# Two attention layers over 64 small graphs: the first step's turn moved from TensorE to VectorE and transfers, and the first loads reordered

## The chip, the core and the metric

The kernel runs on one core of a Trainium2 chip. A core has five engines with instruction streams of their own: TensorE (PE, matrix products and transposes, with PEld its weight loads), VectorE (DVE), ScalarE (ACT), GpSimd (POOL) and SyncE (SP), which here only issues transfers (DMAs). SyncE and ScalarE issue DMAs; 16 DMA engines carry them out. The metric is the device time of one launch in microseconds (us), lower is better. A time is compared as the median of several runs.

## What is computed

Input x holds 64 graphs of 256 nodes with 512 features, all in float32; adj holds a 256 x 256 adjacency of booleans for each graph. Two layers follow each other, both of the form x = x + attention(relu(layernorm(x))).

```
# layer 0: 4 heads of 64
h = relu(layernorm(x)); q, k, v = h @ Wq, h @ Wk, h @ Wv          # 512 -> 256 each
sim = where(adj, q k^T / 8, -max); x = x + softmax(sim) v @ Wo + bo
# layer 1: 8 heads of 64
h = relu(layernorm(x)); h = layernorm(h) * gamma + beta
q, k, v = split(h @ w_qkv.T)                                      # 512 -> 512 each
s = where(adj | eye, q k^T / 8, -1e9); x = x + softmax(s) v @ w_out.T + b_out
```

## The kernel before

**Steps and periods.** `fast_path` works on two graphs at a time: a step has G = 2 graphs of 256 rows, so NT = 4 row blocks of 128 rows, and there are NSTEP = 32 steps. The large products are done by a scheme with seven products for a 2 x 2 block product (`PRODUCT`, `project_qk`, `project_v1`, `combine`); its sums of operands (`act_sums0`, `act_sums1`, `weight_sum`) are made mostly by GpSimd.

**Who sets the order.** Nothing is scheduled automatically: TensorE, VectorE, ScalarE and GpSimd run in the order in which the program emits instructions, and that order is written by hand. `at(period, place, fn, ...)` puts a call at a place on a common scale (a period is 6.4 long, 6.2 where its number is negative), and at the end all events are sorted by place and called (L1496). Each engine takes its instructions from this list in that order, and an instruction that waits holds up all that stand behind it on its engine. SyncE's transfers come in the same order, and SyncE waits in order too. Transfers use eight completion semaphores in turn, so one transfer is issued only when the one eight places before it has landed.

**Start of the kernel.** Steps 0 and 1 are brought in by a path of their own, before the regular rhythm begins:

- `first_loads` (L432) loads x of step 0 in four row blocks with Wq, Wk, the flags of step 0 and Wv. `load_h(1)` (L505) loads step 1's x, 1 MB, into a buffer of the tag "xt" of the pool io.
- `norm0` (L665) takes mean and variance of each row block on VectorE (L647, L648); GpSimd makes the factor r (L677 for step 0, `row_scales` L657 to L659 for the others). `first_scale` (L685) and `scale_row` (L661) apply them on ScalarE (L689, L663). Their place in step 0 is by row block.
- `first_turn` (L791, TensorE) and `first_fill` (L803) turn step 0's h and write the ReLU into hT. Each of the four column chunks is evacuated by ScalarE if even and by VectorE if odd (L807, L809). `first_qk` (L811, L820) projects q and k; VectorE (L827) and ScalarE (L828) evacuate.
- `neighbours` (L581, L587) finds on VectorE which rows have any neighbour (the flags, any_of); `adjacency_cast` (L543) and `adjacency_transpose` (L547) turn the adjacency with TensorE for steps 0 to 2; `neighbours_rows` and `neighbours_turn` (L606, L614) spread the flags.
- **The turn of h.** hT must have the features on the partitions. There are two ways. `transpose_h` (L728) lets TensorE transpose 16 blocks of 128 x 128 (L735), and ScalarE evacuates each chunk with the ReLU (L739). `turn_blocks` (L754) and `move_blocks` (L764) let VectorE transpose 32 x 32 blocks in place (L759, four instructions) and then move the blocks between partitions by 16 transfers of 64 KB issued by SyncE (L771); `place_h` (L773) then applies the ReLU on ScalarE from SBUF (L782, four instructions, each needs all 16 transfers). `by_tensor` (L749) chooses: TensorE for step 0, for step 1 of layer 0 and for the last step of layer 1, the transfers for all others.
- Behind the turn, step 0's attention of layer 0 is done pair by pair (a pair is two heads): `scores` (L1055), `mask_scores` (L1078), `exponentials` (L1083), `weigh` (L1126), `weigh_out` (a copy by ScalarE, L1141). The four score banks of PSUM are used in turn. The sums of each pair's exponentials are made by GpSimd and VectorE (L1090, L1096, L1103), inverted in `key_sums` (L1159), written to DRAM (`line`, L1173, 4 KB) and read back spread over the partitions by `inverse_in` (L1184, two transfers a pair); GpSimd multiplies them in (`normalise`, L1202). `combine_rows` (L1018, L1025) then multiplies with w_o, after both pairs.
- Step 1's first projection (`project_qk`, L902) runs between step 0's pair 0 and its combine.
- **Weights.** `weight_load` (L473) loads w_qkv in three parts (n = 0, 1, 2 for q, k, v; four blocks each of 256 KB in rows of 512 bytes, L481) and w_out (n = 3, one transfer of 1 MB, L478). VectorE turns w_qkv (`weight_turn`, L490), TensorE w_out (`weight_block`, L498). `later_weights` (L451) loads w_o in two transfers (L453) and the two bias rows (L458).

SyncE's order at the start is: step 0's loads, step 1's x, w_q (two blocks), step 1's flags, the rest of w_q, w_k, w_out, w_o in two, b_o, b_out, w_v, line of pair 0, x of step 0 again (xt, L524), the two L1184 of pair 0, x of step 2 (L512), flags of step 2, line of pair 1 and its two L1184.

Of the kernel before, what the change touches and what calls it, by code (L numbers as in the profile page):

```python
# [8 lines left out]
FP = mybir.dt.float32  # L9
# [3 lines left out]
AF = mybir.ActivationFunctionType  # L13
# [305 lines left out]
def fast_path(  # L319
# [21 lines left out]
    nc = tc.nc  # L341
    P = 128
    B, N, D = x.shape
    DH = 64
    G = 2
    NSTEP = B // G
    NIC = N // P
    NT = G * NIC
    T = G * N
    NC = D // P  # L350
# [7 lines left out]
    act = ctx.enter_context(tc.tile_pool(name="act", bufs=1))  # L358
# [73 lines left out]
    def first_loads():  # L432
# [12 lines left out]
        for i in range(2):  # L445
# [2 lines left out]
                wv[:, i * P:(i + 1) * P].rearrange("(c p) o -> p c o", p=P),  # L448
            )

    def later_weights():  # L451
        for i in range(2):
            nc.sync.dma_start(  # L453
                wo0[:, 2 * i:2 * i + 2].rearrange("p j c o -> p (j c) o"),
                wo[:, i * HD:(i + 1) * HD].rearrange("(c p) o -> p c o", p=P),
            )
        for v, t in ((bo, bo_b), (b_out, bout_b)):
            nc.sync.dma_start(t, bass.AP(tensor=v.tensor, offset=v.offset, ap=[[0, P], [1, D]]))  # L458

    def first_gamma():  # L460
        gbr = sm.tile([2 * NC, P], FP, name="gbr", tag="turned_p", bufs=1)
# [223 lines left out]
    def first_scale(t):  # L685
        st = S[0]
        r, mr = st["r"][:, t:t + 1], st["mr"][:, t:t + 1]
        nc.vector.tensor_scalar(mr, st["mean"][:, t, 0:1], r, -1.0, op0=ALU.mult, op1=ALU.mult)
        nc.scalar.activation(st["h"][:, t, :], st["h"][:, t, :], AF.Identity, bias=mr, scale=r)  # L689

# [55 lines left out]

    def by_tensor(s, lyr):  # L749

        return s == 0 or s == (1, NSTEP - 1)[lyr]


    def turn_blocks(s, lyr, t):  # L754

        st = S[s]
        if "blocks" not in st:
            st["blocks"] = act.tile([P, NQ, NC, NT, Q], FP, name="blocks", tag=("turned", "h")[lyr])
        nc.vector.transpose(  # L759
            st["blocks"][:, :, :, t, :].rearrange("p b c n -> p c b n"),  # L760
            st["h"][:, t, :].rearrange("p (c b n) -> p c b n", c=NC, b=NQ),
        )
# [39 lines left out]
    def first_fill(g):  # L802
        for c in range(NC):  # L803
            b0, _, step = B_OF[c // HC]
            dst, src = S[0]["hT"][:, b0 + g * step, c % HC, :], S[0]["ph"][c][:, g]
            if c % 2:
                nc.vector.tensor_scalar(dst, src, 0.0, None, op0=ALU.max)  # L807
            else:
                nc.scalar.activation(dst, src, AF.Relu)  # L809
# [402 lines left out]
    def at(period, place, fn, *args):  # L1212
        events.append((period * (PERIOD if period >= 0 else FIRST) + place, len(events), fn, args))
# [93 lines left out]
    for s in range(NSTEP):  # L1307
# [2 lines left out]
        if s == 1:  # L1310
            p -= 3.93 / FIRST
        if s:
            at(*((-3, 5.71), (-2, 5.3))[s - 1] if s < 3 else (p - 1, AT_H1 + 0.01), load_h, s)
            at(*((-2, 3.2), (-2, 5.35))[s - 1] if s < 3 else (p - 1, 1.3), load_adjacency, s)
        if s < 3:
            at(p, (2.0, 2.4, -5.95)[s], adjacency_cast, s)
            at(p, (3.46, 3.583, -5.825)[s], adjacency_transpose, s)
        else:
            at(p - 1, 4.9, adjacency_pack, s)
        for t in range(NT):  # L1320
            at(p, ((0.5, 0.9, 1.73, 1.74)[t], (1.6995, 1.6996, 2.0295, 2.0296)[t], -6.3 + 0.01 * t)[s] if s < 3 else (0.95, 1.05, 1.2, 1.35)[t], norm0, s, t)
            if s == 0:
                at(p, (0.95, 1.35, 1.745, 2.15)[t], first_scale, t)
            else:
                at(p, (2.375 + 0.001 * t, (-5.8, -5.799, -5.6, -5.599)[t])[s - 1] if s < 3 else 1.6 + 0.001 * t, scale_row, s, t)
            if not by_tensor(s, 0):
                at(p, AT_X - 0.00035 + 0.00001 * t if s > 2 else (2.6, 2.601, 2.72, 2.721)[t], turn_blocks, s, 0, t)
        if not by_tensor(s, 0):
            at(p, AT_X - 0.00031 if s > 2 else 3.0, move_blocks, s)
        for g in range(G):  # L1330
            if s < 3:
                at(p, (1.8, 2.03, -5.8)[s] + 0.001 * g, neighbours, s, g)
            else:
                at(p - 1, AT_Q0 - 0.0009, neighbours, s, g)
        if s < 2:
# [22 lines left out]
        else:  # L1358
            for c in range(NC):
                if by_tensor(s, 0):  # L1360
                    at(p, 2.9292 + 0.0001 * c, transpose_h, s, 0, c)
                else:
                    at(p, AT_Q0 - 0.001 + 0.0001 * c, place_h, s, 0, c)
            at(p, AT_Q0 - 0.0005 if s > 1 else FIRST_C0 + 0.1, lambda s=s: act_sums0(S[s]["hT"]))
            at(p, AT_Q0 - 0.0004 if s > 1 else FIRST_C0 + 0.101, lambda s=s: act_sums1(S[s]["hT"]))
            at_set(p, 3.3 if s < 2 else AT_Q0, SET, project_qk, s, 0, 0)
# [106 lines left out]
    gbr, blocks = [], {}  # L1473
    at(-3, 5.7, first_loads)
    at(-3, 5.705, lambda: gbr.append(first_gamma()))
    at(-2, 4.93, later_weights)
    for i in range(4):
        at(-2, 4.301 if i else FIRST_Q0 + 0.32, weight_sum, nc.gpsimd, wqk0, i)
        at(-1, 1.21, weight_sum, nc.gpsimd, wo0, i)
    for n, place in ((0, 4.0), (1, 4.0), (3, 4.0), (2, 5.0)):  # L1480
        at(-2, place, lambda n=n: blocks.update({n: weight_load(n)}))
    at(-2, FIRST_V0 + 0.2, lambda: gamma_beta(gbr[0]))
    for i in range(12):
        place = (
            4.6395, 4.6396, 4.9, 4.901, 4.902, 5.19965, 5.19966, 5.7, 12.6, 12.601, 12.602, 13.0,
        )[i]
        at(-2, place, lambda i=i: weight_turn(blocks[i // 4], i // 4, i % 4))
    for c in range(4):
# [53 lines left out]
```

## Time and profile before

| what | us |
|---|---|
| median of three runs (lowest, highest) | 3075.1 (3072.61, 3076.8) |
| the profiled execution | 3072.65 |
| its span, first to last instruction | 3070.9 |
| TensorE busy | 3063.4 |
| VectorE, GpSimd, ScalarE busy | 2534.3, 2295.8, 1212.2 |

The profile is that of one execution. Its page gives busy times, the chain of waits that ended last, and groups of instructions by source line (L735 is line 735). The trace answers finer questions: the chain in order of time in a window, the instructions of one engine in order of time, rates of transfer in a window, and how long a transfer took from issue to landing. TensorE's granted clock is full in all slices of the page. Idle time of an engine that is not on the chain costs nothing by itself.

### The profile page before, as it was taken

To read this page: it belongs to the slowest core of one execution; us is meant where nothing else is said; L and a number is where in the kernel's file an instruction comes from. 1 tells how busy PE (TensorE), PEld (TensorE's weight loads), DVE (VectorE), ACT (ScalarE), POOL (GpSimd) and SP (SyncE) were. 2 spreads that over 40 slices of the span, in tenths; PEclk is the share of its full clock that TensorE was granted. 3 is DMA by queue.
4 is the path that set the end of the run, shared out by engine and by line. 5 is a ranking of instruction groups with operands and counts; after the bars stand their busy time and mean duration, and the time that the engine had idled before them with its cause. 6 is when DMAs were issued, how large, how long until landed. Compare 5 with 4: busy or idle time off the path is not lost.

```text
span 3070.9 us, 55407 instructions
## 1 busy us (share of the span) xinstructions
PE 3063.4 (100%) x20106; PEld 2527.4 (82%) x20106; DVE 2534.3 (83%) x4739; ACT 1212.2 (39%) x2133; POOL 2295.8 (75%) x2120
## 2 busy tenths in 40 slices
PE   9999999999999999999999999999999999999999
PEld 7888888888888888888888888888888888888887
DVE  7888888888888888888888888888888888888766
ACT  5443443434343343433444333443434344343431
POOL 6877787777877777777877777787777877778753
PEclk9999999999999999999999999999999999999999
DMA  6223222233222331323323233222232222332311
GB/s 159 58 88 95 78 75 85 74 95 95 60 88 71 100 95 53 91 73 94 95 60 90 74 89 94 75 77 80 81 94 83 72 83 74 101 91 56 92 35 50
DMA packets 192365, 251.20 MB, mean 82 GB/s; under 512 B 58264, under 2 KB 84504, under 8 KB 192088
## 3 DMA queue, kind: packets, MB, share of 16 engines
q1 hardware_dynamic: 128800, 180.46, 20.8%
q10 hardware_dynamic: 63288, 67.15, 7.5%
q8 instruction: 161, 2.64, 0.4%
q14 instruction: 116, 0.95, 0.1%
HBM read 128.59 MB, written 34.34 MB: 53 GB/s over the span
## 4 chain that ended last, share of the span: by engine, by line
PE 100%; DVE 0%; issue 0%; ACT 0%; POOL 0%; POOLq 0%
PE mm L902 38%; PE mm L999 19%; PE mm L983 13%; PE sc L1055 9%; PE sc L1126 6%; PE mm L949 6%; PE mm L1126 5%; PE mm L1055 3%; PE mm L932 1%; PE mm L1025 0%; PE mm L820 0%; PE mm L789 0%; PE mm L735 0%; PE mm L498 0%; PE sc L798 0%; PE mm L553 0%
## 5 line engine op out<-in xcount | busy, mean ns | idle before, releaser
L902 PE MATMUL mm<-hT,wqkv 128*128 128x256 f32 x3584 | 787.4, 380 | 0.0
L902 PEld LDWEIGHTS mm<-hT,wqkv 128*128 128x128 f32 x3584 | 677.9, 190 | 102.6 <-issue 11.4
L1090 POOL TENSOR_TENSOR pd<-p 128x512 f32<-128x512 f32 x383 | 480.1, 1275 | 253.4 <-ACT p L1083 195.5
L999 PE MATMUL mm<-wo,oT 128*128 128x256 f32 x2632 | 578.8, 379 | 0.0
L999 PEld LDWEIGHTS mm<-wo,oT 128*128 128x128 f32 x2632 | 499.7, 190 | 69.2 <-issue 0.7
L1083 ACT ACTIVATE p<-p 128x512 f32<-128x512 f32 x766 | 441.4, 627 | 102.8 <-DVE p L1078 91.1
L1078 DVE TENSOR_TENSOR p<-sc,n 128x512 f32<-128x512 f32 x579 | 363.1, 683 | 113.1 <-PE sc L1055 113.1
L983 PE MATMUL mm<-wqkv,hT 128*128 128x256 f32 x1792 | 395.2, 381 | 0.0
L902 PE MATMUL mm<-hT,wqk 128*128 128x256 f32 x1736 | 383.7, 381 | 0.0
L983 PEld LDWEIGHTS mm<-wqkv,hT 128*128 128x128 f32 x1792 | 337.9, 190 | 55.0 <-issue 10.3
L902 PEld LDWEIGHTS mm<-hT,wqk 128*128 128x128 f32 x1736 | 327.0, 190 | 53.5 <-issue 10.3
L870 POOL TENSOR_TENSOR xt<-xt,u 128x512 f32<-128x512 f32 x183 | 233.1, 1274 | 140.3 <-DVE xt L864 67.4
L1055 PE MATMUL sc<-qk 64*128 64x256 f32 x2320 | 292.7, 385 | 0.0
L1055 PEld LDWEIGHTS sc<-qk 64*128 64x128 f32 x2320 | 217.8, 186 | 59.7 <-issue 27.6
L1096 DVE STREAM_TRANSPOSE turned_p<-pd 128x1024 f32<-128x1024 f32 x192 | 237.2, 1235 | 26.6 <-POOL pd L1090 25.9
L663 ACT ACTIVATE h<-h,mr,r 128x512 f32<-128x512 f32 x252 | 187.9, 806 | 170.0 <-POOL mr L659 170.0
L1202 POOL TENSOR_TENSOR oT<-oT 128x512 f32<-128x512 f32 x188 | 240.2, 1278 | 1.1 <-DMA oT<-line 1.1
L1103 DVE TENSOR_REDUCE part<-turned_p 128x32 f32<-128x1024 f32 x192 | 233.2, 1215 | 4.4
L1126 PE MATMUL sc<-p,v 128*32 128x256 f32 x3152 | 190.8, 382 | 0.0
L949 PE MATMUL mm<-hT,wv 128*128 128x256 f32 x840 | 188.3, 382 | 0.0
L855 ACT COPY u<-mm 128x512 f32<-128x512 f32 x62 | 36.4, 586 | 368.9 <-PE mm L999 221.7
L949 PEld LDWEIGHTS mm<-hT,wv 128*128 128x128 f32 x840 | 156.6, 190 | 26.8 <-ACT vT L836 6.2
(162 smaller groups left out, 4443.9 us busy)
## 6 DMA issues: line engine op xcount, KB each, us to landing
h<-blocks SPq DMA_DIRECT2D x960, 64.0 KB, 2.0
oT<-line SPq DMA_DIRECT2D x376, 128.0 KB, 3.0
h<-in_x_dram SPq DMA_DIRECT2D x31, 1024.0 KB, 5.6
xt<-in_x_dram ACTq DMA_DIRECT2D x60, 512.0 KB, 4.8
out_dram<-xt SPq DMA_DIRECT2D x32, 512.0 KB, 3.1
v<-values ACTq DMA_DIRECT2D x480, 32.0 KB, 1.9
out_dram<-xt ACTq DMA_DIRECT2D x30, 512.0 KB, 4.4
ne<-ne SPq DMA_DIRECT2D x90, 64.0 KB, 2.0
```

The lines of the kernel that those rows point to most:

```text
L902: nc.tensor.matmul(bank[:, k, :], w[:, wa, c, k, a * P:(a + 1) * P], st["hT"][:, ba, c, :], start=first and (k, c) == (0, 0), stop=(k, c) ...
L949: nc.tensor.matmul(bank, wv0[:, wa, c, :], st["hT"][:, ba, c, :], start=first and c == 0, stop=c == HC - 1, skip_group_check=True,)
L983: nc.tensor.matmul(bank[:, t, :], st["hT"][:, ba, c, t * P:(t + 1) * P], wqkv1[:, wa, c, 2, :], start=first and (t, c) == (0, 0), stop=(t, ...
L999: nc.tensor.matmul(bank[:, t, :], oT[:, ba, c, t * P:(t + 1) * P], w[:, wa, c, :], start=first and (t, c) == (0, 0), stop=(t, c) == (NIC - ...
L1055: nc.tensor.matmul(sc[g][e][:, kc, :], qk[rows, 1, k0:k0 + P], qk[rows, 0, g * N:(g + 1) * N], start=True, stop=True,)
L1078: nc.vector.tensor_tensor(p[e][:, g], sc[e], neg[:, :, g, :], ALU.add)
L1083: nc.scalar.activation(p[e][:, g], p[e][:, g], AF.Exp, scale=SCALE)
L1090: nc.gpsimd.tensor_tensor(st["pd"][:, e], p[e][:, :, 0, :], p[e][:, :, 1, :], ALU.add)
L1096: nc.vector.transpose(st["turned_p"], st.pop("pd").rearrange("p e g (b k) -> p (e g b) k", k=32))
L1103: nc.vector.tensor_reduce(st["part", lyr, prs][:, i], st.pop("turned_p"), axis=mybir.AxisListType.X, op=ALU.add)
L1126: nc.tensor.matmul(po[r0:r0 + 32, g, :], (st["v1"][:, g * NIC + kc, pr * P + r0:pr * P + r0 + Q] if lyr else st["v0"][:, r0 // Q, pr, g * ...
L1202: nc.gpsimd.tensor_tensor(dst, dst, invb, ALU.mult)
```

## The change

Step 1's h of layer 0 is turned by VectorE and 16 transfers instead of TensorE (`by_tensor`, the buffer tag in `turn_blocks`, places of `turn_blocks`, `move_blocks`, `place_h`). For that, step 1's statistics and row scales come earlier on VectorE, GpSimd and ScalarE: all four L647 of step 1 directly behind the first evacuation of step 0's q.

SyncE's order becomes: step 0's loads, step 1's x, step 1's flags, w_q (four blocks), w_out, the first block of w_k, the 16 moves, the other three blocks of w_k, b_o, line of pair 0, xt, the two L1184 of pair 0, x of step 2, w_o in one transfer, b_out, flags of step 2, w_v (four blocks), line of pair 1 and its two L1184.

Smaller parts: step 0's flags (any_of, and the cast of its adjacency) come before the statistics of row blocks 2 and 3; row block 1's first scale is split in two halves; the fills of graph 0 are all done by ScalarE; step 1's flags are taken after q and k of step 0; VectorE turns all of w_k after pair 1's masks. GpSimd's row scales of step 1 come before the masks of step 0.

Line numbers above L451 stay; below they move by at most two. The program's order shows the 16 products of L735 gone from that place on TensorE, the four L760 on VectorE and the 16 L772 on SyncE added.

```diff
--- before.py
+++ after.py
@@ -448,14 +448,14 @@
                 wv[:, i * P:(i + 1) * P].rearrange("(c p) o -> p c o", p=P),
             )
 
+    def load_row(v, t):
+        nc.sync.dma_start(t, bass.AP(tensor=v.tensor, offset=v.offset, ap=[[0, P], [1, D]]))
+
     def later_weights():
-        for i in range(2):
-            nc.sync.dma_start(
-                wo0[:, 2 * i:2 * i + 2].rearrange("p j c o -> p (j c) o"),
-                wo[:, i * HD:(i + 1) * HD].rearrange("(c p) o -> p c o", p=P),
-            )
-        for v, t in ((bo, bo_b), (b_out, bout_b)):
-            nc.sync.dma_start(t, bass.AP(tensor=v.tensor, offset=v.offset, ap=[[0, P], [1, D]]))
+        nc.sync.dma_start(
+            wo0[:, :4].rearrange("p (i j) c o -> p i (j c) o", i=2), wo.rearrange("(c p) (i o) -> p i c o", p=P, i=2)
+        )
+        load_row(b_out, bout_b)
 
     def first_gamma():
         gbr = sm.tile([2 * NC, P], FP, name="gbr", tag="turned_p", bufs=1)
@@ -686,7 +686,8 @@
         st = S[0]
         r, mr = st["r"][:, t:t + 1], st["mr"][:, t:t + 1]
         nc.vector.tensor_scalar(mr, st["mean"][:, t, 0:1], r, -1.0, op0=ALU.mult, op1=ALU.mult)
-        nc.scalar.activation(st["h"][:, t, :], st["h"][:, t, :], AF.Identity, bias=mr, scale=r)
+        for cols in (slice(0, D // 2), slice(D // 2, D)) if t == 1 else (slice(0, D),):
+            nc.scalar.activation(st["h"][:, t, cols], st["h"][:, t, cols], AF.Identity, bias=mr, scale=r)
 
 
 
@@ -748,14 +749,14 @@
 
     def by_tensor(s, lyr):
 
-        return s == 0 or s == (1, NSTEP - 1)[lyr]
+        return s == 0 or (s, lyr) == (NSTEP - 1, 1)
 
 
     def turn_blocks(s, lyr, t):
 
         st = S[s]
         if "blocks" not in st:
-            st["blocks"] = act.tile([P, NQ, NC, NT, Q], FP, name="blocks", tag=("turned", "h")[lyr])
+            st["blocks"] = act.tile([P, NQ, NC, NT, Q], FP, name="blocks", tag="h" if lyr or s == 1 else "turned")
         nc.vector.transpose(
             st["blocks"][:, :, :, t, :].rearrange("p b c n -> p c b n"),
             st["h"][:, t, :].rearrange("p (c b n) -> p c b n", c=NC, b=NQ),
@@ -803,7 +804,7 @@
         for c in range(NC):
             b0, _, step = B_OF[c // HC]
             dst, src = S[0]["hT"][:, b0 + g * step, c % HC, :], S[0]["ph"][c][:, g]
-            if c % 2:
+            if g and c % 2:
                 nc.vector.tensor_scalar(dst, src, 0.0, None, op0=ALU.max)
             else:
                 nc.scalar.activation(dst, src, AF.Relu)
@@ -1310,26 +1311,26 @@
         if s == 1:
             p -= 3.93 / FIRST
         if s:
-            at(*((-3, 5.71), (-2, 5.3))[s - 1] if s < 3 else (p - 1, AT_H1 + 0.01), load_h, s)
+            at(*((-3, 5.71), (-2, 5.255))[s - 1] if s < 3 else (p - 1, AT_H1 + 0.01), load_h, s)
             at(*((-2, 3.2), (-2, 5.35))[s - 1] if s < 3 else (p - 1, 1.3), load_adjacency, s)
         if s < 3:
-            at(p, (2.0, 2.4, -5.95)[s], adjacency_cast, s)
+            at(p, (1.727, 2.4, -5.95)[s], adjacency_cast, s)
             at(p, (3.46, 3.583, -5.825)[s], adjacency_transpose, s)
         else:
             at(p - 1, 4.9, adjacency_pack, s)
         for t in range(NT):
-            at(p, ((0.5, 0.9, 1.73, 1.74)[t], (1.6995, 1.6996, 2.0295, 2.0296)[t], -6.3 + 0.01 * t)[s] if s < 3 else (0.95, 1.05, 1.2, 1.35)[t], norm0, s, t)
+            at(p, ((0.5, 0.9, 1.73, 1.74)[t], 1.231 + 0.001 * t, -6.3 + 0.01 * t)[s] if s < 3 else (0.95, 1.05, 1.2, 1.35)[t], norm0, s, t)
             if s == 0:
-                at(p, (0.95, 1.35, 1.745, 2.15)[t], first_scale, t)
+                at(p, (0.95, 1.35, 1.745, 1.80005)[t], first_scale, t)
             else:
-                at(p, (2.375 + 0.001 * t, (-5.8, -5.799, -5.6, -5.599)[t])[s - 1] if s < 3 else 1.6 + 0.001 * t, scale_row, s, t)
+                at(p, (1.7 + 0.001 * t, (-5.8, -5.799, -5.6, -5.599)[t])[s - 1] if s < 3 else 1.6 + 0.001 * t, scale_row, s, t)
             if not by_tensor(s, 0):
-                at(p, AT_X - 0.00035 + 0.00001 * t if s > 2 else (2.6, 2.601, 2.72, 2.721)[t], turn_blocks, s, 0, t)
+                at(p, AT_X - 0.00035 + 0.00001 * t if s > 2 else 2.0295 + 0.0001 * t if s == 1 else (2.6, 2.601, 2.72, 2.721)[t], turn_blocks, s, 0, t)
         if not by_tensor(s, 0):
-            at(p, AT_X - 0.00031 if s > 2 else 3.0, move_blocks, s)
+            at(p, AT_X - 0.00031 if s > 2 else (2.03, 3.0)[s - 1], move_blocks, s)
         for g in range(G):
             if s < 3:
-                at(p, (1.8, 2.03, -5.8)[s] + 0.001 * g, neighbours, s, g)
+                at(p, (1.725, 2.3685, -5.8)[s] + 0.0001 * g, neighbours, s, g)
             else:
                 at(p - 1, AT_Q0 - 0.0009, neighbours, s, g)
         if s < 2:
@@ -1360,7 +1361,7 @@
                 if by_tensor(s, 0):
                     at(p, 2.9292 + 0.0001 * c, transpose_h, s, 0, c)
                 else:
-                    at(p, AT_Q0 - 0.001 + 0.0001 * c, place_h, s, 0, c)
+                    at(p, (AT_Q0 - 0.001 if s > 1 else 2.9292) + 0.0001 * c, place_h, s, 0, c)
             at(p, AT_Q0 - 0.0005 if s > 1 else FIRST_C0 + 0.1, lambda s=s: act_sums0(S[s]["hT"]))
             at(p, AT_Q0 - 0.0004 if s > 1 else FIRST_C0 + 0.101, lambda s=s: act_sums1(S[s]["hT"]))
             at_set(p, 3.3 if s < 2 else AT_Q0, SET, project_qk, s, 0, 0)
@@ -1473,16 +1474,17 @@
     gbr, blocks = [], {}
     at(-3, 5.7, first_loads)
     at(-3, 5.705, lambda: gbr.append(first_gamma()))
-    at(-2, 4.93, later_weights)
+    at(-2, 4.93, load_row, bo, bo_b)
+    at(-2, 5.26, later_weights)
     for i in range(4):
         at(-2, 4.301 if i else FIRST_Q0 + 0.32, weight_sum, nc.gpsimd, wqk0, i)
         at(-1, 1.21, weight_sum, nc.gpsimd, wo0, i)
-    for n, place in ((0, 4.0), (1, 4.0), (3, 4.0), (2, 5.0)):
+    for n, place in ((0, 4.0), (3, 4.01), (1, 4.32), (2, 5.4)):
         at(-2, place, lambda n=n: blocks.update({n: weight_load(n)}))
     at(-2, FIRST_V0 + 0.2, lambda: gamma_beta(gbr[0]))
     for i in range(12):
         place = (
-            4.6395, 4.6396, 4.9, 4.901, 4.902, 5.19965, 5.19966, 5.7, 12.6, 12.601, 12.602, 13.0,
+            4.6395, 4.6396, 4.9, 4.901, 5.345, 5.346, 5.347, 5.348, 12.6, 12.601, 12.602, 13.0,
         )[i]
         at(-2, place, lambda i=i: weight_turn(blocks[i // 4], i // 4, i % 4))
     for c in range(4):
```

## The prediction

> **What bounds the kernel now.** I read the page's busy times first, then the chain of waits, then the chain of the first 66 us, since the diff moves nothing later than that.
>
> ```profile
> PE 3063.4 (100%) x20106; PEld 2527.4 (82%) x20106; DVE 2534.3 (83%) x4739; ACT 1212.2 (39%) x2133; POOL 2295.8 (75%) x2120
> ```
>
> TensorE is busy 3063.4 of 3070.9 us, so 7.5 us of waits are left. A change gains only by taking work off TensorE, and loses by every wait that it puts in front of it. In the chain of 33 to 66 us (start, length, what):
>
> ```profile
> 34.27 1.75 PE mm L735 x16
> 36.02 1.86 PE sc L1126 x32
> 37.88 1.93 PE sc L1055 x16
> 39.81 1.92 PE mm L902 x8
> ...
> 59.00 6.87 PE mm L1025 x16
> ```
>
> L735 is the turn of step 1's h that the change removes, 1.75 us. Then come step 0's pair 0 weighed (L1126), pair 1's scores (L1055), step 1's projection (L902) and, at 59.00, step 0's first combine (L1025). That one needs both pairs of oT normalised by POOL (L1202, the second from 55.67), and POOL needs the inverse sums that SyncE's queue fetches. So I read that queue (start, length of issue):
>
> ```profile
> 32.06 2.06 SPq L481 DMA_DIRECT2D wr<-in_L_gnn_w_qkv_dram  x4
> 37.37 0.33 SPq L1173 DMA_DIRECT2D line<-keys  x1
> 37.81 0.40 SPq L524 DMA_DIRECT2D xt<-in_x_dram  x1
> 40.80 1.15 SPq L1184 DMA_DIRECT2D oT<-line  x2
> 42.00 0.58 SPq L512 DMA_DIRECT2D h<-in_x_dram  x1
> 42.68 0.46 SPq L517 DMA_DIRECT2D ad<-in_adj_dram  x1
> 48.79 0.33 SPq L1173 DMA_DIRECT2D line<-keys  x1
> 50.15 1.09 SPq L1184 DMA_DIRECT2D oT<-line  x2
> ```
>
> The two L1173 lines are alike (4 KB), yet the first comes back only after 3.4 us (L1184 waits until 40.80), the second after 1.3. What differs is the queue: the first stands behind w_v's four blocks, the last of which landed at 39.7. A small transfer thus waits for what was issued before it, and lands about 1.0 after it.
>
> Last, rates and the moves of a later step:
>
> ```profile
> 17.00:26.00 9.00, 9.00 (x43) 7.94 (x42) 6.17 (x15) 2.30 (x5) 6.84 (x10) 1.00 1.24 182
> 28.00:32.00 4.00, 4.00 (x22) 3.01 (x19) 3.63 (x8) 3.33 (x7) 3.74 (x5) 1.00 1.06 369
> 33.00:38.00 5.00, 5.00 (x56) 3.70 (x57) 4.61 (x10) 2.49 (x6) 2.15 (x3) 1.00 1.11 203
> 44.00:48.00 4.00, 4.00 (x43) 2.98 (x44) 3.87 (x7) 2.15 (x4) 4.00 (x4) 1.00 0.96 249
> ```
> ```profile
> 110.01 11.85 SPq L771 DMA_DIRECT2D h<-blocks  x16
> 141.44 10.03 SPq L771 DMA_DIRECT2D h<-blocks  x16
> ```
>
> The last column is GB/s: 182 to 203 while w_qkv's blocks (512-byte rows) flow, 249 to 369 for long rows. Sixteen moves of 64 KB occupy SyncE for 10.0 us or more.
>
> **Part 1, the turn leaves TensorE.** Removed: 16 transposes, 1.75 us, and the four ACT fills behind them (L739, 2.07). Added: four DVE transposes (0.67 each, L759), 16 transfers, four ACT fills from SBUF (L782, same size, taken as 2.1). When the last transfer lands:
> - step 1's h lands at 16.2 (issued 6.92, 9.3 to landing); its place in the queue is unchanged. The four statistics, now ahead of L827's second evacuation, start there: two pairs of 1.69 end at 19.6.
> - POOL's row scales to ACT's start took 2.1 (23.51 to 25.65): 21.7. L663's four rows take 2.94: 24.7. The last DVE transpose ends at 25.4.
> - the last of 16 issues starts 9.4 later (10.03 less one issue of 0.59) and lands 2.0 after: **36.9**. Other end: 38.7, by the burst of 11.85.
>
> What is queued behind that wait on ACT: the order of the program puts the four fills ahead of L1141, the copy of pair 0's weighed sums. Fills end at 39.0, the copy at 39.6. L1055 of pair 1 uses four score banks, and the fourth is the one which L1141 empties; TensorE, there by about 36.8, does five of eight score products and waits. The last three (0.24 each, 1.93/8) end at 40.3, so L902 starts at 40.3 instead of 39.81: **+0.5**. The 1.75 are gone into this wait.
>
> [...]
>
> **Part 2, step 0's flags sooner.** any_of (1.27) leaves its place between the last two mr; the last mr waits then for POOL's r (11.29) and ACT's previous row (11.63), so row 3 is scaled from 11.63, not 12.13: TensorE's idle 0.62 before its turn shrinks by 0.5. The split row and four fills on ACT instead of two and two cost nothing: L820 uses the chunks one after the other, 0.22 per product, and TensorE waits later for row 3 anyway. Without that cover they would cost up to 0.4. The 0.5 is also swallowed by the waits of parts 1 and 3.
>
> **Part 3, loads.** Queue after the moves: w_k's three last blocks, b_o, line 0, xt, two L1184, h of step 2, w_o (512 KB in one), b_out, flags of step 2, w_v's four blocks (they were at 32.06), and only then line 1 (line 0 and line 1 are the inverse sums of step 0's two pairs). Line 1's keys are ready at about 50 (48.76 before, DVE later by w_k's turns), and w_v is still on its way. The sum, by the rates above:
> - w_k 0.79 MB at 203: 3.9, from 36.9 to 40.8; b_o 0.7 at 369: 41.5; line 0 in at 42.5. xt, issued when the fills end (39.0), 1.05 MB, 3.0: 44.5; L1184 0.7: 45.2.
> - h of step 2, 1.05 MB at 369 or 249: 48.0 to 49.4; w_o 1.4; b_out 0.7; flags 0.9 (the 128 KB took about that at 47.5 to 48.9): 51.0 to 52.4.
> - w_v 1.05 MB at 203 or 182: 5.2 to 5.8: **56.2 to 58.2**.
> - line 1 one later, L1184 issued at once; its two last 0.6 + 2.8: 60.6 to 62.6. POOL's L1202 1.27 and 0.1 of handing over: L1025 starts at **62.0 to 64.0** instead of 59.00: +3.0 to +5.0, I take the middle, **+4.0**. This contains the +0.5, and everything gained earlier, since TensorE only arrives earlier at the same wait.
>
> Lesser waits under that cover: DVE's four w_k transposes need w_k at 40.8 and hold n=6's evacuation until about 44.9, some 0.4 late for TensorE; POOL has L642, L912, L410 (8.2 together) behind L1202, done at about 72, before scores at 72.77 + 4. Without the cover, 0.4. One load of w_o saves an issue of 0.6 on SyncE, hidden; w_v is turned near 80, hidden. After 66 TensorE is full and the loss is not won back.
>
> [...] The 512-byte rows ran at half of the long ones. [...]
>
> **Rivals.**
> - *Not slower*: w_v lands before line 1 is issued, or does not hold it, and the moves are in by 33. Then 1.75 + 0.5 are gained: -2.2, 3072.9. For it: 1 MB is 3 us of data at 369. Against: 10 us of issues. It decides when line 1 lands before 54.2 (59.00 less 3.4 and 1.4).
> - *Only the moves count*: line 1 passes w_v, the scores' wait stays: +0.5, 3075.6. Against it: line 0's 3.4.
> - *Clearly slower*: SyncE's moves stretch as in the burst at 110.01 (+1.8; its last transfer also landed 1.5 later after its issue), which pushes w_k and all behind it; with the slow rates +5.0 + 3.3 = +8.3, 3083.4. It decides over +6.2: when w_v's last block lands after 59.4 (65.2 less the 5.8 that follow).
> - *The change does not do what it says*: the program's order shows the 16 transposes gone and the 16 transfers there, so I leave it no chance.
>
> **How the numbers follow.** The profiled execution took 3072.65 (span 3070.9 and 1.75 around it); the median of the three runs is 3075.1. By the profile's own time 3072.65 + 4.0 = 3076.65; against the median, which I predict, 3075.1 + 4.0 = **3079.1**. Chances: forecast (+3 to +5) 0.5, only the moves 0.13, not slower 0.12, clearly slower 0.25. The range takes in -2.2 and +8.3: 3072.9 to 3083.4. Within 0.2% (6.2 us, about what a measurement of this kernel tells from none): the first three, with a little of each taken for error, 0.67; slower 0.3; faster 0.03.
>
> **What would show it.** Right: TensorE idle some 2.8 in L1055 near 37 to 40, released by ACT's L1141; 16 issues from about 25.4 to 35.4; line 1 issued after w_v and back only near 57 to 59; TensorE idle some 3 at L1025, released by POOL's L1202; nothing different after 80. Wrong: L1025 starting at 57 to 59, or line 1 back within 2 us of its issue; or waits after 70, where I count none.

## The result and the profile after

| | before | after |
|---|---|---|
| median of 15 runs each (lowest, highest), us | 3073.02 (3072.45, 3076.8) | 3080.27 (3077.03, 3083.72) |
| the profiled execution; its span | 3072.65; 3070.9 | 3079.95; 3078.2 |

The changed kernel takes 1.0023 times as long (95% interval 1.0015 to 1.0031), 7.25 us more by the medians and 7.30 by the profiled executions. The page's first row, TensorE and the others:

```profile
PE 3065.1 (100%) x20090; PEld 2526.2 (82%) x20090; DVE 2536.0 (82%) x4741; ACT 1210.9 (39%) x2136; POOL 2292.2 (74%) x2120
```

Sixteen instructions fewer (the turn; in the timeline of before 1.84 lie between its start and the next group's), and yet TensorE is busy 1.7 longer; span less busy, its idle time, grew from 7.5 to 13.1. Most of both is found in one place. TensorE's instructions in order of time, those with a wait, the products behind the second wait and the combine (start, length; in brackets the idle time ahead and what ended it):

```profile
38.46 1.13 PE L1056 MATMUL sc<-qk 64*128 64x256 f32 x6 [1.21 <-DVE p L1079]
...
46.76 2.41 PE L903 MATMUL mm<-hT,wqk 128*128 128x256 f32 x8 [2.19 <-DVE qk L839]
48.96 0.63 PE L618 MATMUL mm<-identb,rows 128*128 128x128 bf16 x4
49.53 2.94 PE L1127 MATMUL sc<-p,v 128*32 128x256 f32 x32
...
62.47 1.02 PE L1026 MATMUL mm<-wo,oT 128*128 128x512 f32 x2
66.27 6.28 PE L1026 MATMUL mm<-wo,oT 128*128 128x512 f32 x14 [2.78 <-POOL oT L1203]
```

The same places in the kernel before:

```profile
12.99 0.66 PE L798 MATMUL sc<-ident,h 128*128 128x128 f32 x4 [0.62 <-ACT h L689]
...
44.76 1.99 PE L902 MATMUL mm<-hT,wqk 128*128 128x256 f32 x8
46.59 0.39 PE L618 MATMUL mm<-identb,rows 128*128 128x128 bf16 x4
46.90 1.93 PE L1126 MATMUL sc<-p,v 128*32 128x256 f32 x32
...
58.84 7.03 PE L1025 MATMUL mm<-wo,oT 128*128 128x512 f32 x16
```

Three waits, 6.18 in all; before had none in this stretch, but one of 0.62 near 13 that is gone, which leaves the 5.6 by which idle time grew. Behind the combine TensorE is 6.67 later than before, at its last instruction 7.50; the 0.8 between come in steps of at most 0.4 beyond 700 us. e1 and e9 (below) lose 0.7 and 1.0 there, and the cause is open. The combine (L1026, before L1025) did two matmuls and waited for pair 1's oT. In the kernel before it ran through from 58.84 in this view (59.00 in the chain). The windows after the second wait (the column ahead of the last two is the granted clock):

```profile
46.00:49.00 3.00, 2.24 (x9) 1.72 (x10) 2.96 (x4) 0.10 (x1) 1.26 (x2) 0.87 0.85 236
49.00:52.00 3.00, 3.00 (x33) 1.54 (x35) 2.51 (x10) 0.58 (x1) 3.00 (x4) 0.56 1.06 362
```

The clock, as the mean of a window, falls to 0.56, and the 32 products of L1127 take 2.94 instead of 1.93; with L903 (2.41 for 1.99) and L618 (0.63 for 0.39) that is 1.7 more, about as much as the turn's 16 transposes had taken. Groups that a wait cuts in two also count longer here (L1056 1.56 and 1.13 instead of 2.00), since a matmul's end is modelled. The second wait is for VectorE, which turns w_k (L490) when it has landed, makes a sum of operands (L410) and only then evacuates (L839):

```profile
42.25 2.49 DVE L490 STREAM_TRANSPOSE wqkv<-wr 128x512 f32<-128x512 f32 x4 [1.75 <-DMA wr<-in_L_gnn_w_qkv_dram]
44.66 1.45 DVE L410 TENSOR_TENSOR wqkv<-wqkv 128x512 f32<-128x512 f32 x1
46.03 0.68 DVE L839 TENSOR_TENSOR qk<-mm,qk 128x512 f32<-128x512 f32 x1
```

SyncE's queue answers to the one shown of before:

```profile
35.04 1.68 SPq L481 DMA_DIRECT2D wr<-in_L_gnn_w_qkv_dram  x3
...
43.07 1.13 SPq L1185 DMA_DIRECT2D oT<-line  x2
44.30 0.53 SPq L512 DMA_DIRECT2D h<-in_x_dram  x1
44.88 0.70 SPq L455 DMA_DIRECT2D wo<-in_L_gnn_Wo_dram  x1
...
47.23 7.22 SPq L481 DMA_DIRECT2D wr<-in_L_gnn_w_qkv_dram  x4
54.54 0.95 SPq L1174 DMA_DIRECT2D line<-keys  x1
60.77 1.70 SPq L1185 DMA_DIRECT2D oT<-line  x2
```

Line 1's 4 KB (the second L1174; its keys were done at 51.0) are issued at 54.54, when SyncE is done with issuing w_v's four blocks (7.22, in before 2.06), and read back from 60.77. Before, that pair of times was 48.79 and 50.15. The chain of waits goes through it:

```profile
54.54 6.21 DMA line<-keys
...
61.31 3.51 DMA oT<-line
...
64.95 1.27 POOL oT L1203
...
66.27 6.28 PE mm L1026 x14
```

So there are two delays side by side: TensorE comes to the combine 3.6 later than before (62.47), and the line lets it go on only at 66.27.

### The profile page after: what moved, and what is told of

It is laid out like the page before. It is cut to its first block, busy times and chain, and to the rows that moved or that the text cites. A ratio compares the mean times of both kernels' runs of the same rounds, so it can differ in the third digit from the quotient of the medians.

```text
span 3078.2 us, 55408 instructions
## 1 busy us (share of the span) xinstructions
PE 3065.1 (100%) x20090; PEld 2526.2 (82%) x20090; DVE 2536.0 (82%) x4741; ACT 1210.9 (39%) x2136; POOL 2292.2 (74%) x2120
## 4 chain that ended last, share of the span: by engine, by line
PE 97%; DMA 1%; DVE 1%; POOL 0%; SPq 0%; issue 0%; DVEq 0%; POOLq 0%
PE mm L903 37%; PE mm L1000 18%; PE mm L984 13%; PE sc L1056 9%; PE mm L950 6%; PE sc L1127 6%; PE mm L1127 5%; PE mm L1056 3%; DMA h<-in_x_dram 1%; PE mm L1026 0%; DMA line<-keys 0%; PE mm L933 0%; POOL wqk L410 0%; DVE bs L647 0%; PE mm L736 0%
## 5 line engine op out<-in xcount | busy, mean ns | idle before, releaser
L903 PE MATMUL mm<-hT,wqkv 128*128 128x256 f32 x3584 | 787.4, 380 | 0.0
L903 PEld LDWEIGHTS mm<-hT,wqkv 128*128 128x128 f32 x3584 | 678.0, 190 | 102.5 <-issue 11.4
L1079 DVE TENSOR_TENSOR p<-sc,n 128x512 f32<-128x512 f32 x579 | 363.0, 682 | 112.6 <-PE sc L1056 112.6
L903 PE MATMUL mm<-hT,wqk 128*128 128x256 f32 x1736 | 384.2, 381 | 2.2 <-DVE qk L839 2.2
L903 PEld LDWEIGHTS mm<-hT,wqk 128*128 128x128 f32 x1736 | 327.1, 190 | 55.7 <-issue 10.3
L1056 PE MATMUL sc<-qk 64*128 64x256 f32 x2320 | 293.3, 385 | 1.2 <-DVE p L1079 1.2
L1056 PEld LDWEIGHTS sc<-qk 64*128 64x128 f32 x2320 | 218.0, 186 | 61.4 <-issue 27.2
L1127 PE MATMUL sc<-p,v 128*32 128x256 f32 x3152 | 191.8, 383 | 0.0
```

The lines of the kernel that those rows point to most:

```text
L903: nc.tensor.matmul(bank[:, k, :], w[:, wa, c, k, a * P:(a + 1) * P], st["hT"][:, ba, c, :], start=first and (k, c) == (0, 0), stop=(k, c) ...
L1056: nc.tensor.matmul(sc[g][e][:, kc, :], qk[rows, 1, k0:k0 + P], qk[rows, 0, g * N:(g + 1) * N], start=True, stop=True,)
L1079: nc.vector.tensor_tensor(p[e][:, g], sc[e], neg[:, :, g, :], ALU.add)
L1127: nc.tensor.matmul(po[r0:r0 + 32, g, :], (st["v1"][:, g * NIC + kc, pr * P + r0:pr * P + r0 + Q] if lyr else st["v0"][:, r0 // Q, pr, g * ...
```

## Experiments

The times of e1 to e12 stand beside runs of the kernel before on the same chip (median 3072.6 to 3072.8); a trace is of one execution. "Reads" is when SyncE issues the reads of line 1 (the last thing that needs the line); "reached" is TensorE's first matmul of step 0's combine, "goes on" its third one where a wait stands between.

| run | reads | reached | goes on | median us | ratio to before [95%] |
|---|---|---|---|---|---|
| before | 50.15 | 58.84 | | | |
| after | 60.77 | 62.47 | 66.27 | 3080.27 | 1.0023 [1.0015, 1.0031] |
| e1_wv_last | 54.13 | 59.56 | | 3074.08 | 1.0005 [0.9996, 1.0014] |
| e2_wk_ahead | 60.79 | 60.50 | 65.97 | 3083.31 | 1.0035 [1.0022, 1.0049] |
| e3_wk_ahead_wv_last | 59.30 | 62.09 | 65.28 | 3079.33 | 1.0022 [1.0012, 1.0032] |
| e4_before_wv_late | 54.40 | 58.95 | | 3073.90 | 1.0006 [0.9997, 1.0015] |
| e5_no_turn | 56.69 | 58.41 | 61.65 | 3075.31 | 1.0010 [1.0001, 1.0019] |
| e6_wk_turned_late | 59.03 | 61.66 | 65.11 | 3079.35 | 1.0021 [1.0012, 1.0030] |
| e7_wv_last_masks_first | 55.00 | 61.44 | | 3076.52 | 1.0012 [1.0003, 1.0021] |
| e8_wk_ahead_masks_first | 55.70 | 62.18 | 66.35 | 3083.66 | 1.0035 [1.0022, 1.0049] |
| e9_masks_first_wk_in_gap | 55.44 | 59.82 | | 3074.27 | 1.0005 [0.9996, 1.0014] |
| e10_e9_wo_early | 53.32 | 60.55 | | 3074.59 | 1.0009 [1.0000, 1.0018] |
| e11_after_wo_early | 57.84 | 62.19 | | 3077.47 | 1.0017 [1.0007, 1.0026] |
| e12_wk_early_turned_early | 55.71 | 60.19 | | 3075.73 | 1.0010 [1.0001, 1.0019] |

The theory: line 1 queues behind w_v, and with it TensorE's combine. The first rival: the 16 DMA engines are full whatever the order. A second question came from the trace of after: whether the 2.19 us wait (w_k late, VectorE late with it) is a loss of its own.

**e1_wv_last**, w_v behind the line:

```diff
-    for n, place in ((0, 4.0), (3, 4.01), (1, 4.32), (2, 5.4)):
+    for n, place in ((0, 4.0), (3, 4.01), (1, 4.32), (2, 7.0)):
```

> The changed kernel with w_v's four blocks behind step 0's second line of sums on SyncE's queue (one of the four still ahead of the two reads of the line, L1185). Theory (the line queues behind w_v, 57.2 to 60.6): the line lands near 55 instead of 60.76, the reads by 59 to 60, and TensorE's first L1026 is no longer held by GpSimd's oT but only by what its own queue lost to the 2.19 us wait and the low clock behind it: it starts at 62 to 63 (66.27 in the changed kernel, 59.00 before), so the profiled time is 3 to 4.5 us under that of the changed kernel, near 3076. Rival (the DMA engines as a whole are too full in 43 to 61, so whichever load stands last, the reads are late): L1026 starts at 65 or later, within 1.5 us of the changed kernel.

TensorE's waits and its combine:

```profile
38.36 1.13 PE L1056 MATMUL sc<-qk 64*128 64x256 f32 x6 [1.80 <-DVE p L1079]
...
45.47 1.99 PE L903 MATMUL mm<-hT,wqk 128*128 128x256 f32 x8 [1.01 <-DVE qk L839]
...
59.56 7.03 PE L1026 MATMUL mm<-wo,oT 128*128 128x512 f32 x16
```

The line's reads go out 6.6 earlier, and the wait for oT is gone: w_v ahead of the line is the cause that ends last in the changed kernel, and the rival falls. The trace of the changed kernel speaks against the rival too (the last two columns are the DMA engines' busy share and GB/s):

```profile
55.00:58.00 3.00, 3.00 (x16) 2.66 (x15) 1.20 (x4) 2.79 (x5) 2.83 (x4) 1.00 1.11 173
58.00:61.00 3.00, 3.00 (x22) 2.60 (x21) 2.13 (x4) 0.06 (x1) 1.19 (x3) 1.00 0.20 36
```

In the last 3 us before the line was read the engines were on average a fifth busy; the line, issued at 54.54, still came in only behind w_v's last block. The size was wrong in the good direction, 59.56 instead of 62 to 63. Up to about 47 us the two programs are the same, but here w_k was in at 41.07 and not at 42.12, the second wait is 1.01 and not 2.19, and the clock stays at 1.00. So not all of e1's gain is w_v's place. The time is not told apart from before.

**e2_wk_ahead** and **e3_wk_ahead_wv_last**, w_k ahead of the 16 moves; e3 also has w_v's place at 7.0, as in e1:

```diff
-    for n, place in ((0, 4.0), (3, 4.01), (1, 4.32), (2, 5.4)):
+    for n, place in ((0, 4.0), (3, 4.01), (1, 4.02), (2, 5.4)):
```

> The changed kernel with all four w_k blocks ahead of the 16 moves on SyncE's queue (three stood behind them). Theory (w_k in at 42.12 made VectorE turn it late, and that gave TensorE's 2.19 us wait for step n=6's evacuation; w_v makes L1026 late on its own): the 2.19 us wait shrinks under 0.5 us and the granted clock stays near 1.0 in 46 to 52; the moves land 1 to 2.5 us later (near 38.5); line 1 is still behind w_v, with about 1 to 4 us less ahead of it, so L1026 starts at 62 to 65 and the profiled time is 1 to 4 us under that of the changed kernel, and still 2 to 5 over that of before. Rival (w_k's late turns are the whole loss): L1026 starts by 59.5 and the time is that of before.

> Both orders at once: w_k ahead of the moves, and w_v behind the second line (one block still ahead of its reads). Theory (two causes: late w_k and w_v ahead of the line): neither the 2.19 us wait nor the wait for oT is left; L1026 starts at 58.5 to 60 and the time is that of before within 1 us (3072 to 3074), so the turn by transfers itself costs nothing and gains nothing. Rival (the moves, the one-piece load of w_o or the flags cost by themselves): L1026 starts at 61 or later, 2 us or more over before.

Both expectations failed. The 2.19 wait did go, but nothing was won. SyncE's waits in e2, from 30 to 50:

```profile
SPq L524 <- DVE wqkv L490: 4.9, 1, 4.9
```

With w_k's buffer taken earlier, step 0's x (xt) gets the buffer that w_k holds until VectorE has turned it (42.15), and SyncE waits 4.9 with everything behind it, though line 0 had landed at 39.78. So these two runs do not tell what w_k's place alone is worth. Nor does e3 put w_v behind the line: its first block was issued at 48.12, ahead of the line (52.80), and landed at 59.07, the second stood ahead of the line's reads, and these are still late (59.30).

**e4_before_wv_late**, the kernel before with w_v alone moved:

```diff
-    for n, place in ((0, 4.0), (1, 4.0), (3, 4.0), (2, 5.0)):
+    for n, place in ((0, 4.0), (1, 4.0), (3, 4.0), (2, 5.4)):
```

> The kernel before, with only w_v's four blocks moved behind step 2's h and flags and ahead of the second line of sums, as the changed kernel has them; no other edit. Theory (w_v ahead of the line is a cause by itself): the line lands 2 to 4 us later than in the kernel before, TensorE's first combine starts at 60 to 62 instead of 59.00 and waits for GpSimd's oT, the time is 1 to 3 us over before (3074 to 3076). Rival (the line is late only in company with w_k and w_o behind the moves): the combine starts within 0.5 us of 59.00 and the time is that of before.

The line is read 4.25 later than in before, as the theory has it, but TensorE does not notice. GpSimd's product of pair 1:

```profile
58.52 1.27 POOL L1202 TENSOR_TENSOR oT<-oT 128x512 f32<-128x512 f32 x1 [2.69 <-DMA oT<-line]
```

It ends at 59.79, just when the combine, begun at 58.95, needs it; in before it ended at 56.94. The kernel before had some 3 us of slack there, and w_v ahead of the line uses all of it and no more. As the cause of a loss w_v's place needs company: here the rival was right.

**e5_no_turn**, the turn back on TensorE, all other orders as changed (`by_tensor` and the tag as before):

```diff
-        return s == 0 or (s, lyr) == (NSTEP - 1, 1)
+        return s == 0 or s == (1, NSTEP - 1)[lyr]
```

> The changed kernel with step 1's h of layer 0 turned on TensorE again, as in the kernel before: no turn on VectorE and no 16 moves; every other order of the change stays, w_v ahead of the second line included. Theory (the moves hold SyncE's queue for 10.1 us and with it w_k, line 0 and everything behind; TensorE gains about 2 us by the turn): w_k lands by 36, the 2.19 us wait and the wait for VectorE's first mask are gone; w_v and the second line land some 4 us earlier than in the changed kernel, near 56.5, so the first combine starts at 59 and its third matmul at 61 to 62.5: the time is 1 to 3 us over before, 4 to 6 under the changed kernel. Rival (the moves are beside the point, the order of the other loads alone makes the line late): the line lands at 60 or later and the time is within 1.5 us of the changed kernel.

```profile
58.41 1.02 PE L1026 MATMUL mm<-wo,oT 128*128 128x512 f32 x2
61.65 7.97 PE L1026 MATMUL mm<-wo,oT 128*128 128x512 f32 x14 [2.22 <-POOL oT L1203]
```

As the theory had it: reads at 56.69, the combine goes on at 61.65, +2.5 by the medians. After the wait the clock fell (0.73 as the mean of 60 to 65), and the 14 products took 7.97 instead of 6.28. Read with e4, this adds the line's delay up: 50.15 before; 54.40 with w_v ahead (+4.25); 56.69 with the other orders of the change too, w_o and the output's bias above all (+2.3); 60.77 with the moves, and w_k behind them (+4.1).

**e6_wk_turned_late**, w_k turned behind pair 1's sums:

```diff
-            4.6395, 4.6396, 4.9, 4.901, 5.345, 5.346, 5.347, 5.348, 12.6, 12.601, 12.602, 13.0,
+            4.6395, 4.6396, 4.9, 4.901, 5.871, 5.872, 5.873, 5.874, 12.6, 12.601, 12.602, 13.0,
```

> The changed kernel with VectorE's four turns of w_k put behind pair 1's sums, so that nothing on VectorE waits for w_k; all loads as in the changed kernel. Theory (two waits in a row, of which only the last, for oT, sets the end): the 2.19 us wait is gone, the granted clock stays at 1.0 in 46 to 52, TensorE comes to L1026 some 3 us earlier, at 59 to 60, and waits longer there; the line is still issued behind w_v at 54 to 55 and lands near 60.7, L1026 goes on at 65.5 to 66.5: the time is that of the changed kernel within 1 us. Rival (the wait for the evacuation and the low clock are part of the loss): L1026 goes on at 64 or earlier, the time is 2 us or more under that of the changed kernel.

The time is the changed kernel's, and the combine is again released by oT: the second wait does not set the end while the line is late. The equal time is a sum, though: the line was read 1.7 sooner (59.03), and the clock fell behind the wait in the combine (0.66 as the mean of 65 to 70; 7.97 for its 14 products). TensorE, however, came to the combine only 0.8 sooner: the turns, now from 50.65 to 53.14, held the next evacuations instead, and waits of 0.45 and 1.87 for VectorE took the place of the 2.19.

**e7_wv_last_masks_first**, **e9_masks_first_wk_in_gap**, **e10_e9_wo_early**: w_v last (as e1), and pair 1's first masks ahead of pair 0's sums:

```diff
+            elif (s, lyr, prs) == (0, 0, (0,)):
+                turned = sums = period, w + 0.00004
...
-            at(period, w + (0.05 if (s, lyr, prs) == (NSTEP - 1, 1, (0, 2)) else -0.00008), inverse_in, s, lyr, prs)
+            at(period, w + (0.05 if (s, lyr, prs) == (NSTEP - 1, 1, (0, 2)) else 0.00005 if (s, lyr, prs) == (0, 0, (0,)) else -0.00008), inverse_in, s, lyr, prs)
```

with w_k's turns at 5.871 to 5.874 (e7) or at 5.8561 to 5.8564 (e9, e10), and in e10 `at(-2, 4.015, later_weights)`.

> The kernel with w_v behind the second line, with two further moves on VectorE: w_k's turns behind pair 1's sums, and the first masks of pair 1 ahead of pair 0's sums. Theory (the turn frees TensorE of about 2 us, and VectorE's order took them back as waits of 1.80 us for the mask and 1.01 us for the evacuation): both waits are under 0.4 us, the first combine starts at 56.8 to 58, its third matmul when pair 1's oT is ready, at 57.5 to 59 (59.56 with w_v last alone, 58.84 before); the time is 0 to 1.3 us under before and 1 to 2.5 under the kernel with w_v last alone. Rival (VectorE and the line are the bound, TensorE only waits at another place): the third matmul of the combine starts at 59.5 or later, and the time is that of the kernel with w_v last alone.

> The kernel with w_v last and pair 1's first masks ahead of pair 0's sums, with w_k's four turns (2.49 us) moved from behind pair 1's sums into the 2.13 us in which VectorE waited for GpSimd's pd. Theory (VectorE's order, not its amount of work, took the turn's 2 us back): the waits of 0.80 and 1.87 us for VectorE's evacuations are gone, none over 0.6 us is left before the combine, which starts at 57.6 to 58.8 (61.44 with the turns behind the sums, 59.56 with w_v last alone); the time is within 1 us of before. Rival (VectorE is full in 36 to 57, so that 2.8 us of added turns must show somewhere): waits for VectorE of 1.5 us or more in sum stay, the combine starts at 59.5 or later, the time is 1.5 us or more over before.

> As the kernel beside it, with w_o and the output's bias loaded ahead of the moves, where the kernel before had them. In the changed kernel the DMA engines were half busy while the moves were issued, and the second line stood behind 2.5 us of w_o and bias. Theory: the second line lands within 2 us of its issue, pair 1's oT is ready by 57.5, the combine starts at 57.2 to 58.8 without a wait; 0 to 1.5 us under before. Rival (what is loaded ahead of the moves delays them, and with them the projections): the last move lands after 37.5 and the combine starts at 59 or later; over before.

e7 failed. The wait for the mask fell from 1.80 to 0.35, as intended, but w_k's turns cost 0.80 and 1.87 at the later evacuations (0.45 and 1.87 in e6). In e9 the turns stand in VectorE's gap. TensorE's waits there:

```profile
37.40 1.13 PE L1056 MATMUL sc<-qk 64*128 64x256 f32 x6 [0.35 <-DVE p L1079]
...
44.15 0.66 PE L498 MATMUL mm<-ident,wr 128*128 128x128 f32 x4 [0.63 <-ACT wo L500]
...
55.79 1.97 PE L903 MATMUL mm<-hT,wqk 128*128 128x256 f32 x8 [0.97 <-DVE qk L843]
```

Together 1.95, about the 1.84 that L735's 16 transposes had taken in before. The combine starts at 59.82 and the median is 1.5 over before: nearer to e9's rival than to its theory, though the interval does not tell it from before. Only 1.32 of the waits are for VectorE, so that the rival's reason (VectorE is full) is a part of it; ScalarE shows as well. e10 brings the line's reads to 53.32, the earliest of all runs but before, and gains nothing: h of step 2 landed later (52.5, w_k's four blocks now all behind the moves), its statistics hold an evacuation, TensorE waits 1.84 there and starts the combine at 60.55. Its moves were not delayed (last landed 36.76), against the rival's reason.

**e8_wk_ahead_masks_first** and **e12_wk_early_turned_early**: w_k ahead of the moves, w_v at 7.0, masks first; as in e3, w_v's first block then stands ahead of the line (issued at 44.85 and 46.41, landed at 55.38 and 55.49), and the line is read just behind it (55.70 and 55.71). e8 has xt's load at 5.27 and the turns at 5.871 to 5.874; e12 has xt as changed and turns w_k at 4.902 to 4.9023, so that its buffer is free early.

> As the kernel of the run beside it (w_v behind the second line, w_k's turns late, masks first), and w_k ahead of the 16 moves, with step 0's x loaded behind the reads of line 0, so that these do not wait for w_k's turns in SyncE's order. Theory (with w_k ahead, nothing is left in the queues when the moves end, so h of step 2, w_o and the lines start some 4 us earlier): line 0 lands near 39 to 41, the second line within 2 us of its issue, third matmul of the first combine at 57 to 58.5; the time is 0.3 to 1.8 us under before. Rival (the moves start late behind w_k and hold TensorE before the projections): a wait of 1.5 us or more stands ahead of step 1's first projection between 36 and 44, and the time is over before.

> w_v last, masks first, and w_k both loaded ahead of the moves and turned by VectorE ahead of pair 0's sums (it waited 2 us for GpSimd there). Theory (with nothing large behind the moves, line 0 lands within 2 us of its issue, so the loads behind it begin 2 to 3 us earlier than in the changed kernel, and VectorE has no w_k between masks and evacuations): no wait over 0.6 us before the combine, which starts at 57 to 58.8; 0 to 1.8 us under before. Rival (moves that start behind w_k's 1 MB land 1 us later and GpSimd's sums of h hold the projections): waits ahead of step 1's projections of over 1 us between 36 and 46, and the time is over before.

e8 failed for a reason of neither theory nor rival: its xt (step 0's x for the residual sum) stood behind w_o and h of step 2 and landed at 53.16, GpSimd's sum of it and the bias (L537) waited 6.55 for it, and pair 0's and pair 1's products stand behind that on GpSimd (the second at 65.04). In e12 SyncE no longer waits for w_k, yet line 0 took 3.3 from issue to landing (39.11 to 42.37) and not 2. Waits of 0.65 and 1.03 for the fills and GpSimd's sums of h stand ahead of the projections, since the last move landed at 38.01 instead of 36.45. That is the rival's mechanism at about its size; the combine starts at 60.19.

**e11_after_wo_early**, the changed kernel with w_o and the output's bias ahead of the moves again:

```diff
-    at(-2, 5.26, later_weights)
+    at(-2, 4.015, later_weights)
```

> The changed kernel with one thing undone: w_o and the output's bias loaded ahead of the moves again (which sends w_k's first block behind them), w_v still ahead of the second line. Theory (each load that the change put ahead of the second line counts with its own time, w_o and bias with 2.9 us): the second line lands at 57.5 to 58.5 instead of 60.76, the combine's third matmul starts at 63 to 64 instead of 66.27; the time is 2 to 3.5 us under the changed kernel. Rival (w_k's later end gives the same back, w_k being in at 43.5 instead of 42.1): the combine's third matmul starts at 65 or later.

```profile
46.48 3.12 PE L903 MATMUL mm<-hT,wqk 128*128 128x256 f32 x8 [2.11 <-DVE qk L839]
...
62.19 7.03 PE L1026 MATMUL mm<-wo,oT 128*128 128x512 f32 x16
```

As expected, the reads come 2.9 sooner (57.84), by w_o's and the bias's own time. Now the wait for oT is gone, and the other delay shows by itself: TensorE reaches the combine at 62.19, 3.35 later than before, after waits of 1.31 and 2.11 and a clock of 0.72 in 45 to 50. The time is 2.8 us under the changed kernel by the medians (the intervals of the two overlap) and 4.7 over before.

No version run here is faster than the kernel before; e1, e4 and e9 are not told apart from it, and e10's interval begins at 1.0000. None of them keeps the turn and is rid of both delays, so what the turn is worth without them stays open.

## Why the prediction was right, and where not

The direction and the mechanism were right, and the time lies in the range. The size was not: the forecast gave +4.0, the result is +7.25. That 3079.1 stands near 3080.27 is luck: the three runs on which it was built had a median of 3075.1, 2.1 above that of the 15 runs.

- **The turn and its moves.** Right: 16 issues from 24.89 to 34.99, the last move in at 36.45 (forecast 25.4 to 35.4, 36.9).
- **The scores' wait.** TensorE stopped where forecast, after five of eight score products, but the step that named the releaser failed: not ACT's copy (L1142, done only near 39.4, when TensorE had gone on at 38.46), but VectorE's first mask of pair 1 (L1079), behind pair 0's sums. I had taken the bank that the copy empties; the program uses another one. L903 starts at 39.52, 0.2 sooner than before, and not 0.5 later. That the gain of the turn goes into a wait was right. e7 and e9 take this wait away, and the gain is then lost at other evacuations and fills: with the turn moved, the waits between 24 us and the combine were 1.95 or more in every run.
- **The flags.** The wait of 0.62 went, as forecast, and was swallowed.
- **The loads up to w_v: the term that was mis-sized.** From the last move to w_v's last block 5.4 MB had to flow. The prediction's sum gives them 20.3 us (36.9 to 57.2), 264 GB/s; they took 24.1 (36.45 to 60.59), 222 GB/s. w_k was 1.3 late; most was lost between 43 and 49: the reads of line 0 were forecast in at 45.2 and were in at 48.1 to 48.3. They shared the engines with xt's 1 MB (issued at 39.00) and h of step 2 (44.30); that this held them is read from the order of issue and not tested. Then h of step 2 was in at 51.90 (48.0 to 49.4), w_o at 53.59 and the bias at 54.85 (51.0 to 52.4), w_v at 60.59 (56.2 to 58.2). w_v itself took 5.7 after the bias, 183 GB/s, within the forecast's rates, but not as one steady flow: 173 GB/s in 55 to 58, then 36 in 58 to 61 with the engines 0.20 busy, a tail that a sum of bytes by a rate does not have. With the engines 1.11 busy the 512-byte rows flowed at 173 GB/s, against 369 with 1.06 busy in the kernel before's row of 28 to 32. Each of these blocks also fills only 32 partitions, and no run tells the two apart.
- **Line 1 behind w_v.** Right: it landed 0.2 after w_v (1.0 forecast), reads and product then took 5.5 (4.8 forecast). 66.27 instead of 62 to 64.
- **The lesser wait.** Forecast as 0.4 late for n=6's evacuation; measured 2.19, and 1.7 more by the clock that fell after it. w_k came 1.3 later than forecast (42.12), and the 2.49 of its turns and 1.45 of L410 stand ahead of the evacuation; in e1, where w_k was in 0.3 later than forecast, the wait is still 1.01. In the changed kernel the cover holds (e6: the same time); without it TensorE comes to the combine 3.35 later (e11), not 0.4.
- **The rivals.** The point from which I let *clearly slower* decide, w_v's last block after 59.4, was passed, and +7.25 lies nearer to its +8.3 than to +4.0. Half of its cause was right (the slow rates), half was not (the moves did not stretch: 10.10 as in the calm row). *Only the moves count* fell with the line's 6.21. *Not slower* did not come, and even with the line early (e1, e9) the 2.2 us gain did not: I had priced TensorE's saving without asking who is next when it arrives sooner.

## What to carry to other kernels

Before you put a load ahead of a small transfer that somebody needs, find the slack of that transfer (here 3 us) and add up everything that then stands ahead of it in bytes and at the rate of a busy stretch (here 222 GB/s), not piece by piece at the rates of quiet ones (which gave 264). Work taken off the busiest engine is a gain only if the engines that feed it there are ahead of it; look at who releases its next instructions, and follow the order of that engine (and the buffers it takes) before counting the gain. Two delays that run side by side hide one another: undo each alone, and the one that ends last shows itself.

## What the runs showed of the hardware

- **The clock after a wait.** After waits of TensorE of 2.11 (e11), 2.19 (the changed kernel), 2.22 (e5), 2.41 (e3), 2.42 (e6), 3.15 (e8) and 4.46 us (e2) the granted clock fell: as the mean of a window to 0.72 (e11, 45 to 50), 0.56 (the changed kernel, 49 to 52), 0.73 (e5, 60 to 65), 0.75 (e3, 38 to 43), and in 65 to 70 to 0.66 (e6), 0.57 (e8) and 0.50 (e2). Where the wait stood in the combine its 14 matmuls took 7.97 to 9.32 instead of 6.28. After waits of 2.17 (e3) and 2.78 (the changed kernel) it did not fall (1.00 in 65 to 70 both times), and after none of up to 1.87, so the length of the wait alone does not tell. In the changed kernel's trace the clock is 0.50 from 48.21 to 51.62, that is for 3.41 us, and 1.00 on both sides; it next changes at 3075.83, behind TensorE's last instruction, 886 times 3.413 us later. In e2 and e8 it stayed low for about twice as long (8.94 and 9.32 for the 14 matmuls). Cut into stretches of 3.41 us, counted from where the clock fell (in the experiments placed by the means of the windows, an estimate), the traces show 1.97 (the changed kernel) to 3.03 us (e2) of TensorE's idle time in the stretch just ahead of each of the seven falls before 80 us, and 1.87 or less in the others at full clock: the 2.17 is cut into 1.27 and 0.91, the 2.78 into 1.79 and 0.99. A stretch at 0.50 was followed by another one when it held idle time itself (0.66 in e8, 1.42 in e2). This is read from single traces, and no run moved a wait to test it.
- **A transfer of 4 KB** took 1.3 us from issue to landing with hardly anything else in flight (line 0 in e5, 37.19 to 38.53) or with the last loads in at 49.07 and 49.55 (line 1 before, 48.79 to 50.13), and 6.2 behind w_v, where its landing followed that of the last load by 0.2.
- **The same program does not land the same way twice**: with identical instructions up to about 47 us, w_k was in at 42.12 in the changed kernel and at 41.07 in e1 (7.1 and 6.1 after the first of its last three issues; 6.1 to 6.4 in e6, e7 and e9), and with it came a wait with a fall of the clock in the one and without in the other. These are single executions; how often each comes is not shown. The changed kernel's runs spread over 6.7 us, e1's over 1.6.
